# Stage two of a four-stage convolution and state-space kernel: chunks of 128 and 64 channels, norm factors through DRAM, B products on two engines

## The chip, the core and the metric

The kernel runs on one core of a Trainium2 chip. The metric is device time in microseconds; the time before is the median of three runs. A core has five engines with a queue of their own each: TensorE (PE, with its weight loads listed as PEld), VectorE (DVE), ScalarE (ACT), GpSimd (POOL) and SyncE (SP), which here issues the DMAs. A queue is worked off in order, so an instruction that waits holds up those behind it.

## The reference, cut to what matters

Four layers follow each other on an image batch of 4 x 192 x 64 x 64, all in f32. Layer 0 is a pair of Mambas, layer 1 (stage two of the kernel) is the one that the change touches, layers 2 and 3 are a dynamic depthwise convolution and a windowed mixing layer (stage three).

```python
def _mamba(xf, ...):                        # 384 inner channels, 16 states
    xm, z = split(xf @ in_proj_w.T)
    xm = silu(causal_depthwise_conv(xm, taps=3))
    dt, B, C = split(xm @ x_proj_w.T)       # 12, 16, 16
    delta = softplus(dt @ dt_proj_w.T + dt_proj_b)
    A = -exp(A_log)
    h = exp(delta * A) * h + (delta * xm) * B      # a scan over the 4096 positions
    y = (h * C).sum(states) + xm * Dskip
    return (y * silu(z)) @ out_proj_w.T

def _L1_conv_ref(x, ...):
    t = _ln(x, over the 192 channels)
    x1 = x + _mamba(t)
    dw = depthwise_conv_3x3(x1)
    x2 = x1 + gelu(batch_norm(dw))
    t = _ln(x2, over the 192 channels)
    h = gelu(t @ mlp_w1.T + mlp_b1)         # 768 hidden channels
    return x2 + h @ mlp_w2.T + mlp_b2
```

## The kernel before

The kernel has three stages. `two_mambas` is layer 0, `mamba_block` is layer 1, and `conv_and_windows` is layers 2 and 3; the end of stage two overlaps with the beginning of stage three. The first two stages are written on the same classes, `Mamba`, `Scans` and `Behind`.

**Units and tiles.** Stage two works in 32 units, 4 images of 8 tiles of T = 512 positions (8 rows of an image). The 192 channels lie as two chunks of CP = 96 on 96 partitions each: a tile of x is [96, 2, 512], and every product over channels is two products of 96 rows, added in PSUM, or gives two outputs of 96 rows.

**The scan.** A unit has 384 x 16 = 6144 state rows, that is 12 groups `k` of 4 tiles of 128. `Scans.step` issues one tile after the other, 48 in a unit, and between two tiles gives `Behind.tick` the turn. For a group: `load` fetches dtE and dtxE from DRAM in four broadcasts each (`load` is called 8 or 12 tiles ahead); `product` multiplies dtxE by B, one instruction of 128x2048, on DVE with B in PSUM (L561); `decay` makes dA = exp(A dt) on ACT in PSUM, two tiles ahead (L568); `step` is the scan on DVE (L574); `read` saves the state after the group's last tile (on POOL, L589) and multiplies h by C on POOL (L590); `sum` adds over the states on PE with outputs of 32 rows, four side by side (L599). There are three buffers of h, so DVE's product for a group waits until the sum of the third group before it is done. In stage one `shared = (3, 7, 11)` makes three of the twelve products on POOL instead, from a copy of B in SBUF (`Bs`), into buffers of their own (`h_apart`), copies the state on ACT, and lets the sums come two tiles later. In stage two `shared` is empty.

**The planner.** `Behind` places the rest of a unit's work between the scan tiles. It has four lanes of generators that yield a `Piece`: its estimated PE time, how many ticks to wait, what must be done before, whether it needs a PSUM bank (there are two, `BANKS`), whether it is a burst on ACT (allowed at the end of a group before a DVE product), and a lock shared by the two norms. Each tick may spend up to 2.1 us of PE work in stage two. What comes out of PSUM is issued one tick (ACT) or two ticks (DVE) after its product. So the program's order on every engine is fixed when the kernel is built.

**The work of a unit.** Lane 1 has `front` of the next unit (in_proj, L452; the convolution of 3 taps as products, L470; x_proj, L486; dt, L496, softplus, dt times xc on POOL, L506, and the stores to DRAM; z) and then `norm` of the one after. Lane 0 has `back`: out_proj (L1011), the addition of x on DVE (L1020) into a strip with a border, [96, 2, 10, 66]. Lane 2 has `tail`: the 3x3 convolution as nine products with diagonal weights per chunk (L1049), batch norm on the way out of PSUM (L1058), Gelu, the addition of x1 on POOL (L1072), and the second norm. Lane 3 has `end`: the MLP (L359, L364, L378) and the last addition (L1084) with its sums for stage three.

**The norm** (`NormT.run`): PE makes the mean on all partitions, DVE subtracts it (L292), ACT squares, PE makes the variance of 128 positions at a time as a column [128, 4] (L304), ACT and POOL raise it to the power -1/2 (L315, L316), PE spreads it over the partitions with the identity (`rb`, L322), DVE multiplies (L330), ACT applies gain and offset (L337).

Of the kernel before, what the change touches and what calls it, by code (L numbers as in the profile page):

```python
# [21 lines left out]
NB = 4  # L22
C = 192
# [70 lines left out]

def paired(a):

    return np.stack([a[:128], np.concatenate([a[128:], a[128:]]), a[:128]], axis=1)
# [67 lines left out]
class Piece:  # L165
# [4 lines left out]
    def __init__(self, pe=0.0, wait=0, after=(), burst=False, bank=False, lock=False):  # L170
        self.pe, self.wait, self.after, self.burst = pe, wait, after, burst
        self.bank, self.lock = bank, lock


class Behind:
# [39 lines left out]
    def try_lane(self, n, edge, force=False, idle=True):  # L215
# [7 lines left out]
        if not all(h[0] for h in p.after) or (p.bank and self.held >= self.BANKS):  # L223
            return None
# [44 lines left out]
class NormT:  # L269


    FIRST = dict(pe=1.7, bank=True)

    def __init__(self, nc, const, work, behind):
        self.nc, self.work, self.behind = nc, work, behind
        self.mean_w = const.tile([CP, CP], F32, name="mean_w")
# [8 lines left out]
    def run(self, x, g, b, d, which):  # L285
        nc, behind = self.nc, self.behind
        nq = T // 128
        mean = behind.bank([CP, T], "mean")
        for k in range(2):
            nc.tensor.matmul(mean, self.mean_w, x[:, k, :], start=(k == 0), stop=(k == 1))  # L290
        h = behind.later(
            lambda: nc.vector.tensor_tensor(  # L292
                d, x, mean.unsqueeze(1).broadcast_to([CP, 2, T]), ALU.subtract
# [4 lines left out]
        sq = self.work.tile([CP, 2, T], F32, name="ln_sq", bufs=1)  # L298
        nc.scalar.activation(sq, d, AF.Square)
        yield Piece(2.5, wait=2, bank=True)  # L300
        var = behind.bank([128, nq], "var")
        for q in range(nq):
            for k in range(2):
                nc.tensor.matmul(  # L304
                    var[:, q : q + 1],
                    sq[:, k, bass.ts(q, 128)],
                    self.mean_w[:, 0:1],
# [3 lines left out]
        behind.locked = False  # L311
# [7 lines left out]
        yield Piece(1.3, after=[h], wait=4, bank=True)  # L319
        rb = behind.bank([CP, T], "rb")  # L320
        for q in range(nq):
            nc.tensor.matmul(  # L322
                rb[:, bass.ts(q, 128)],
                rs[:, q : q + 1].to_broadcast([128, CP]),
                self.ident,
                start=True,
                stop=True,
            )
        h = behind.later(
            lambda: nc.vector.tensor_tensor(  # L330
                d, d, rb.unsqueeze(1).broadcast_to([CP, 2, T]), ALU.mult
            ),
            dve=True,
        )
        yield Piece(after=[h], wait=3)
        for k in range(2):
            nc.scalar.activation(  # L337
                d[:, k, :], d[:, k, :], AF.Identity, scale=g[:, k : k + 1], bias=b[:, k : k + 1]
            )


class MlpT:


# [4 lines left out]
    def run(self, x, taken, last):  # L349
        nc, behind = self.nc, self.behind  # L350
        made = []
        for m in range(NH):
# [1412 lines left out]
```

## Time and profile before

| | us |
|---|---|
| median of three runs (10863.65 to 10865.74) | 10863.88 |
| the profiled execution | 10868.44 |
| its span | 10866.7 |
| busy: PE | 9179.8 (84%) |
| busy: DVE | 9098.4 (84%) |
| busy: POOL | 7032.3 (65%) |
| busy: ACT | 6566.6 (60%) |

These are means over stages with different limits, so they are read by stage: stage one ends at about 5340 us, stage two's scans run from 5435 to 8957 us, and stage three goes on to the end. In a line of a group of instructions stand the line of the code, the engine, the operation, what is written and read, the count, then busy time and mean ns of one, then the engine's idle time just before them with what ended it. PEclk is the share of TensorE's full clock that was granted.

### The profile page before, as it was taken

The page shows a single profiled execution, that of the slowest core. Times are in us where ns is not written, and L with a number is a line of the kernel's source. Part 1 is how long each engine was busy: PE and PEld are TensorE (multiplying, and loading weights), DVE is VectorE, ACT ScalarE, POOL GpSimd, SP SyncE. Part 2 cuts the span into 40 slices and gives each one's busy share as a digit, 9 for nine tenths or more (in the row PEclk, how much of TensorE's full clock was granted, in tenths as well). Part 3 has the DMA queues.
Part 4 walks back from the last instruction along what each step waited for, and adds up shares of the span by engine and source line. Part 5 has one row for each costly group of instructions (what it writes and reads, how often), then busy time and mean ns, then how long its engine had stood idle before and what let it go on. Part 6 is the DMA issues. An engine that isn't in the chain of part 4 may idle for free. (4 is left out here: it accounts for less than half of the span.)

```text
span 10866.7 us, 97590 instructions
## 1 busy us (share of the span) xinstructions
PE 9179.8 (84%) x31352; PEld 3644.1 (34%) x31352; DVE 9098.4 (84%) x7962; ACT 6566.6 (60%) x9784; POOL 7032.3 (65%) x2688
## 2 busy tenths in 40 slices
PE   6888878888887887887679999999999987889898
PEld 2222222222322222222223333333333333455555
DVE  7999999999999999999698888888888885555552
ACT  5666666666666666666466666656666663444443
POOL 5888888888888888888666656656656661111100
PEclk7777777777777777777678889889889887999999
DMA  5666666666666666666454545445444443122110
GB/s 158 177 181 180 177 177 183 175 176 182 177 177 179 177 178 179 176 178 180 128 151 135 140 127 143 133 125 141 129 134 133 133 121 82 41 50 64 42 40 18
DMA packets 969560, 1515.13 MB, mean 139 GB/s; under 512 B 244346, under 2 KB 277150, under 8 KB 968534
## 3 DMA queue, kind: packets, MB, share of 16 engines
q1 hardware_dynamic: 968190, 1505.85, 51.4%
q8 instruction: 247, 4.05, 0.2%
q10 hardware_dynamic: 856, 3.05, 0.1%
q14 instruction: 267, 2.19, 0.1%
HBM read 1295.45 MB, written 213.12 MB: 139 GB/s over the span
## 5 line engine op out<-in xcount | busy, mean ns | idle before, releaser
L574 DVE TENSOR_TENSOR_SCAN h<-dA,m_state,h 128x512 f32<-128x512 f32 x3840 | 4668.9, 1266 | 487.4 <-ACT dA L568 422.7
L590 POOL TENSOR_TENSOR h<-h,C 128x2048 f32<-128x2048 f32 x960 | 4345.4, 4531 | 621.6 <-ACT m_state L587 480.7
L568 ACT ACTIVATE dA<-dtE,m_A 128x512 f32<-128x512 f32 x4608 | 3106.1, 687 | 1332.9 <-DVE h L574 1227.8
L561 DVE TENSOR_TENSOR h<-dtxE,B 128x2048 f32<-128x2048 f32 x960 | 2170.6, 2261 | 78.6 <-DMA dtxE<-r_dtx 65.9
L599 PE MATMUL y<-h,gather 128*32 128x512 f32 x7680 | 1281.3, 746 | 422.9 <-POOL h L590 345.2
L452 PE MATMUL ps_in<-xT,m_in_w 96*128 96x512 f32 x1536 | 939.5, 759 | 258.6 <-ACT raw L455 127.1
L1300 POOL TENSOR_TENSOR d<-d,rs 128x512 f32<-128x512 f32 x64 | 86.8, 1357 | 1589.7 <-DVE rs L1299 1569.1
L470 PE MATMUL ps_conv<-raw,m_conv 128*128 128x512 f32 x2112 | 989.3, 617 | 1.7 <-ACT xc L475 1.7
L574 DVE TENSOR_TENSOR_SCAN h_apart<-dA,m_state,h_apart 128x512 f32<-128x512 f32 x768 | 922.3, 1260 | 40.0 <-ACT dA L568 40.0
L590 POOL TENSOR_TENSOR h_apart<-h_apart,C 128x2048 f32<-128x2048 f32 x192 | 870.2, 4532 | 39.7 <-ACT m_state L587 38.0
L561 POOL TENSOR_TENSOR h_apart<-dtxE,Bs 128x2048 f32<-128x2048 f32 x192 | 889.6, 4633 | 6.0 <-ACT Bs L550 6.0
L452 PEld LDWEIGHTS ps_in<-xT,m_in_w 96*128 96x128 f32 x1536 | 351.3, 241 | 827.2 <-issue 420.5
L589 POOL COPY m_state<-h 128x4 f32<-128x4 f32 x384 | 72.3, 188 | 849.5 <-DVE h L574 813.5
L470 PEld LDWEIGHTS ps_conv<-raw,m_conv 128*128 128x128 f32 x2112 | 417.9, 202 | 599.0 <-issue 562.4
L1049 PE MATMUL ps_dw<-strip,dw 96*96 96x512 f32 x1152 | 578.7, 650 | 1.3 <-ACT x L1058 0.9
L599 PEld LDWEIGHTS y<-h,gather 128*32 128x32 f32 x7680 | 164.7, 117 | 1225.4 <-POOL h L590 552.0
L506 POOL TENSOR_TENSOR raw<-dt,xc 128x1536 f32<-128x1536 f32 x96 | 330.0, 3437 | 294.6 <-ACT dt L505 294.6
L486 PE MATMUL ps_x<-xc,m_pack 128*44 128x512 f32 x576 | 351.0, 758 | 199.5 <-ACT xc L482 194.6
L1465 PE MATMUL sed_ps<-xn,sed 64*128 64x256 f32 (+3 forms) x2944 | 485.9, 404 | 7.0 <-DVE y L1484 7.0
L568 ACT ACT_TABLE_LOAD x345 | 442.6, 1283 | 28.5 <-DMA dtE<-r_dt 22.3
L452 PE MATMUL ps_in<-xn,m_in_w 96*128 96x512 f32 x768 | 399.0, 666 | 47.4 <-ACT z L455 31.2
L378 PE MATMUL ps_o<-hid,t 128*96 128x512 f32 x768 | 390.4, 647 | 34.3 <-ACT hid L371 13.0
(193 smaller groups left out, 12217.1 us busy)
## 6 DMA issues: line engine op xcount, KB each, us to landing
dtE<-r_dt SPq DMA_DIRECT2D x2304, 256.0 KB, 5.0
dtxE<-r_dtx SPq DMA_DIRECT2D x2304, 256.0 KB, 4.1
r_dt<-dt SPq DMA_DIRECT2D x96, 768.0 KB, 4.0
r_dtx<-raw SPq DMA_DIRECT2D x96, 768.0 KB, 5.4
x<-x SPq DMA_DIRECT2D x64, 384.0 KB, 3.9
img<-x SPq DMA_DIRECT2D x28, 512.0 KB, 8.2
xt<-in_x SPq DMA_DIRECT2D x32, 384.0 KB, 5.8
x<-o SPq DMA_DIRECT2D x32, 384.0 KB, 5.0
```

Of the source, the lines that this page charges most:

```text
L378: nc.tensor.matmul(ps, self.w2[:, m, bass.ts(k, CP)], h[:, m, :], start=(m == 0), stop=(m == NH - 1),)
L452: nc.tensor.matmul(ps, self.in_w[:, k, bass.ts(e, 128)], xn[:, k, :], start=(k == 0), stop=(k == 1))
L470: nc.tensor.matmul(ps, self.conv[:, d, j, :], raw[:, d, j : j + T], start=(j == 0), stop=(j == K - 1))
L486: nc.tensor.matmul(ps, self.x_w[:, d, :], xc[:, d, :], start=(d == 0), stop=(d == ND - 1))
L506: nc.gpsimd.tensor_tensor(dtx, dt, xc, ALU.mult)
L561: engine.tensor_tensor(h, u["rows", k // 2, 1], u[B, k % 2].unsqueeze(1).broadcast_to([128, 4, T]), ALU.mult)
L568: self.nc.scalar.activation(dA, u["rows", k // 2, 0][:, j, :], AF.Exp, scale=self.A[:, k, j : j + 1])
L574: self.nc.vector.tensor_tensor_scan(h[:, j, :], u.pop(("dA", k, j)), h[:, j, :], self.state[:, k, j : j + 1], ALU.mult, ALU.add,)
L590: nc.gpsimd.tensor_tensor(h, h, u["C", k % 2].unsqueeze(1).broadcast_to([128, 4, T]), ALU.mult)
L599: self.nc.tensor.matmul(u["ys"][32 * j : 32 * j + 32, :], self.ex.gather[:, i // 2, :], h[:, j, :], start=(i == 0), stop=(i == 3 and not s ...
L1049: nc.tensor.matmul(ps, dw[:, k, j, :], s[:, k, dy : dy + rows, dx : dx + HW], start=(j == 0), stop=(j == 8),)
L1465: nc.tensor.matmul(out, sed[p, int(h is not None), i ^ position(k, s), cols], xn[b, g][p, c, :], start=group(t) not in begun, stop=left[gr ...
```

## The change

All of it is in stage two, but for the layout of three small inputs of stage three (the sums, `pooled` and `w1`, which follow the new chunks).

- The channels lie in chunks of 128 and 64. Inputs of a product hold the second chunk twice, on partitions 0 to 63 and on 64 to 127, so that two products over it can run on the two halves of the rows (`side_by_side`: in_proj, mlp1). Outputs and images hold it folded: the first 256 positions on partitions 0 to 63 and the others on 64 to 127 (`narrow`: out_proj, mlp2; the 3x3 convolution takes 256 columns for that chunk). A pair takes both PSUM banks at once, and `Piece.bank` becomes a number.
- The norm works in place. Its factors go from POOL to DRAM as a row of 512 and come back broadcast to 128 partitions; POOL multiplies by them instead of DVE, and the lock is held until then.
- `shared` is (3, 7, 11) with `folds=True`: POOL makes three of twelve B products, into one buffer of h_apart; the state is copied on ACT, and the sums come two tiles later. D, the gate and the skip stay as they were in stage two.
- x is loaded with its second chunk twice, into two buffers, after `front`; `back` loads x again, folded, into the strip and adds out_proj's result to it. Four small copies on ACT fill the border of the folded half. x2 goes to DRAM folded and comes back as xn with its second chunk twice.

```diff
 class NormT:
...
-        behind.locked = False
         rs = self.work.tile([128, nq], F32, name="ln_rs", tag=f"ln_rs{which}", bufs=1)
...
         h = behind.later(power)
-        yield Piece(1.3, after=[h], wait=4, bank=True)
-        rb = behind.bank([CP, T], "rb")
-        for q in range(nq):
-            nc.tensor.matmul(
-                rb[:, bass.ts(q, 128)],
-                rs[:, q : q + 1].to_broadcast([128, CP]),
-                self.ident,
...
+        yield Piece(after=[h], wait=4)
+        row = self.dram.tile([1, T], F32, name="r_rs", bufs=3)
+        nc.sync.dma_start(row.rearrange("o (q p) -> p (o q)", p=128), rs)
+        yield Piece(wait=2)
+        rb = self.work.tile([128, T], F32, name="rb", bufs=1)
+        nc.sync.dma_start(rb, row.broadcast_to([128, T]))
+        yield Piece(wait=2)
+        nc.gpsimd.tensor_tensor(x, x, rb.unsqueeze(1).broadcast_to([128, 2, T]), ALU.mult)
+        behind.locked = False
+        yield Piece(wait=3)
...
+def side_by_side(nc, outs, wts, x):
+    for o, wt in zip(outs, wts):
+        nc.tensor.matmul(o, wt[:, 0, :], x[:, 0, :], start=True, stop=False)
+    for i, (o, wt) in enumerate(zip(outs, wts)):
+        p = slice(64 * i, 64 * i + 64)
+        nc.tensor.matmul(o, wt[p, 1, :], x[p, 1, :], start=False, stop=True)
+
+def narrow(nc, ps, wt, x, k, start, stop):
+    if k == 0:
+        nc.tensor.matmul(ps, wt[:, :128], x, start=start, stop=stop)
+        return
+    for i in range(2):
+        nc.tensor.matmul(
+            ps[64 * i : 64 * i + 64, :], wt[:, 128:], x[:, bass.ts(i, T // 2)], start=start, stop=stop
+        )
...
     def product(self, u, k):
         apart = k in self.shared
         if apart:
-            h = self.work.tile([128, 4, T], F32, name="h_apart", bufs=2)
+            h = self.work.tile([128, 4, T], F32, name="h_apart", bufs=1 if self.folds else 2)
...
         mamba = Mamba(
-            nc, "m", 3, m_in, const, work, fixed, scan, psum_y, psum_a, dram, ln.ident, ex, behind
+            nc, "m", 3, m_in, const, work, fixed, scan, psum_y, psum_a, dram, ln.ident, ex, behind,
+            (3, 7, 11), True,
         )
...
+        STRIP = ((0, rows), (rows + 2, rows // 2))
+        PART = (slice(0, T), slice(T, T + T // 2))
+        def thrice(dma, a, k):
+            for p, ch, of in ((slice(0, 128), slice(0, 128), None), (half[0], slice(128, C), 0), (half[1], slice(128, C), 1)):
+                rows_of = a[ch, :] if k == 0 or of is None else a[ch, bass.ts(of, T // 2)]
+                dma(p, int(of is not None), rows_of)
...
         def front(u):
-            yield from mamba.front(u["xn"], u["t"] == 0, u["m"])
+            yield from mamba.front(u["x"], u["t"] == 0, u["m"])
+            if u["next"]:
+                load(u["next"])
...
         def back(u):
-            s = strips[b, t] = work.tile([CP, 2, rows + 2, HW + 2], F32, name="strip", bufs=3)
+            s = strips[b, t] = work.tile([128, 3 * rows // 2 + 4, HW + 2], F32, name="strip", bufs=3)
+            thrice(
+                lambda p, k, r: nc.sync.dma_start(
+                    inner(s, k)[p], r.rearrange("p (r c) -> p r c", c=HW)
+                ),
+                a,
+                1,
             )
...
                         lambda k=k, ps=ps: nc.vector.tensor_tensor(
-                            s[:, k, 1 : rows + 1, inside],
-                            ps.rearrange("p (r c) -> p r c", c=HW),
-                            u["x"][:, k, :].rearrange("p (r c) -> p r c", c=HW),
-                            ALU.add,
+                            inner(s, k), inner(s, k), ps.rearrange("p (r c) -> p r c", c=HW), ALU.add
                         ),
...
             yield Piece(after=made)
+            nc.scalar.copy(s[half[1], at, inside], s[half[0], at + n, inside])
+            nc.scalar.copy(s[half[0], at + n + 1, inside], s[half[1], at + 1, inside])
...
-            yield Piece(1.7, bank=True, wait=4, after=[taken[0]])
-            xn = work.tile([CP, 2, T], F32, name="xn2", tag="xn2", bufs=1)
-            yield from ln.run(x2, w["ln2_g"], w["ln2_b"], xn, 2)
+            yield Piece(wait=3)
+            r = dram.tile([C, T], F32, name="r_x2", bufs=2)
+            thrice(lambda p, k, a: nc.sync.dma_start(a, x2[p, PART[k]]), r, 1)
+            yield Piece(wait=2, after=[taken[0]])
+            xn = work.tile([128, 2, T], F32, name="xn2", bufs=1)
+            thrice(lambda p, k, a: nc.sync.dma_start(xn[p, k, :], a), r, 0)
+            yield Piece(1.7, bank=True, wait=2)
+            yield from ln.run(xn, w["ln2_g"], w["ln2_b"], 2)
...
-            u["next"] = units[n + 3] if n + 3 < len(units) else None
+            u["next"] = units[n + 2] if n + 2 < len(units) else None
```

## The prediction

> **What bounds the kernel now.** The chain of waits does not help: it ends in stage three and covers 5% of the span. I therefore read the engines' busy time stretch by stretch, found the stage the change touches, and then asked of that stage the groups of instructions, the waits and the order of time. Stage two starts with the first scan at 5435 us and its last scan ends at 8957 us; the second line below is stage two and the first a piece of stage one, which runs the same scans in another mixture.
>
> ```profile
> 2000.00:5000.00 3000.00, 2457.42 (x7600) 843.36 (x7600) 2919.41 (x2347) 2042.26 (x3295) 2650.95 (x737) 0.77 0.65 178
> ...
> 5435.00:8957.00 3522.00, 3195.92 (x9560) 1179.48 (x9560) 2978.04 (x2319) 2220.83 (x2944) 2179.55 (x1170) 0.88 0.49 134
> ```
>
> The columns are stretch, length, busy time (and instructions) of PE, PEld, DVE, ACT and POOL, granted clock, DMA share, GB/s. Stage two has 32 units (4 images of 8 tiles of 512 positions), so one unit lasts 3522/32 = 110.1 us and keeps PE busy for 99.9, DVE for 93.1, ACT for 69.4, POOL for 68.1 and the DMA engines for 0.49 x 110.1 = 54 us. Two engines are nearly full, PE the fuller. In stage one DVE is 97% busy beside a POOL at 88%: the scans can run that tight where PE has room.
>
> ```profile
> L574 DVE TENSOR_TENSOR_SCAN h<-dA,m_state,h 128x512 f32<-128x512 f32 x1525 | 1871.9, 1268 | 384.7 <-ACT dA L568 358.7 <-DVE h L561 0.5
> L590 POOL TENSOR_TENSOR h<-h,C 128x2048 f32<-128x2048 f32 x381 | 1726.3, 4531 | 30.8 <-POOL m_state L589 0.2
> L561 DVE TENSOR_TENSOR h<-dtxE,B 128x2048 f32<-128x2048 f32 x381 | 861.2, 2260 | 12.7 <-PE y L599 12.7
> L330 DVE TENSOR_TENSOR xn<-xn,rb 96x1024 f32<-96x1024 f32 x61 | 73.2, 1199 | 11.0 <-PE rb L322 11.0
> L364 ACT ACTIVATE hid<-ps_h,t 128x512 f32<-128x512 f32 x178 | 121.1, 684 | 145.3 <-PE ps_h L359 145.3
> L1058 ACT ACTIVATE x<-ps_dw,bn_t,bn_s 96x512 f32<-96x512 f32 x60 | 46.4, 773 | 155.6 <-PE ps_dw L1049 155.6
> ```
>
> These are groups of 5455 to 8955 us (31.8 units): busy, mean ns, idle before. DVE's idle time, 110.1 - 93.1 = 17.0 us a unit, is mostly 358.7/31.8 = 11.3 us before scans that wait for ACT's dA; and ACT is late because in its queue stand copies out of PSUM that wait for PE (145.3 and 155.6 in these two rows alone, 9.5 us a unit). So the end of a unit is set by PE and DVE together, with ACT between.
>
> ```profile
> 6513.60 5.45 PE L452 MATMUL ps_in<-xn,m_in_w 96*128 96x512 f32 x12
> ...
> 10206.08 1.66 PE L1275 MATMUL mean<-x,ones 128*128 128x256 f32 x8
> ...
> 10208.30 2.81 PE L1551 MATMUL ps_o<-hid,t_bw 128*64 128x256 f32 x24
> ```
>
> In the order of time, a product in f32 is two passes. Twelve passes of 512 columns take 5.45 us; the weight loads between them are 0.43 us apart, which is the pass at full clock. Stage three already packs as the change does: 24 passes of 128*64 with 256 columns take 2.81 us, 12 x 0.215 = 2.58 and 0.23 more, so two run at once. The mean has four passes of 128 rows and four of 64 rows: six turns of 0.215 make 1.29, and 0.37 is left for two changes of tile shape, 0.15 to 0.19 each.
>
> **What the Trainium skill says.** (1) TensorEngine Tiling (Array Packing), Key Properties: different tiles work in parallel, and changing the tiling mode drains the engine. The three lines above agree, at 0.15 to 0.19 us a change. (2) The same page, Gotcha 1: row tiles write to different PSUM banks; here a pair therefore takes both of the two banks. (3) SBUF — State Buffer, Who interferes with whom: a DVE instruction with two SBUF inputs contends with GpSimd's reads. Scans and B products read one operand from PSUM, and the scan takes 1260 to 1266 ns in stage one beside a full POOL against 1268 here, so a fuller POOL should not slow DVE. (4) DMA: Bandwidth & Descriptors, Rules for kernel authors: a DMA that reads what another wrote waits for that one's semaphore. So the factors' way through DRAM is two landings in series; the trace has no such pair of this size.
>
> **Part by part, a unit.** DVE loses 3 B products (3 x 2.26 = 6.8) and the two multiplications by rb (2 x 1.20 = 2.4). The last addition of back and of end has 256 columns instead of 512: half of 0.69 and of 0.73, 0.7 together. DVE: 93.1 - 9.9 = 83.2.
>
> POOL gains 3 B products at stage one's 4.635 (13.9), two multiplications of 128x1024, half of L590's 4.531 (4.5), and loses 12 copies of the state at 0.188 (2.3) and half of one L1072 of 1.18 (0.6). POOL: 68.1 + 15.5 = 83.6. That is now as much as DVE.
>
> ACT gains the 12 state copies at stage one's 0.196 (2.4), one copy of Bs (0.585) and four small strip copies (nearest row, POOL's at 0.29: 1.2); its eviction of dw and its Gelu shrink by 0.6. ACT: 69.4 + 3.6 = 73.0, hidden as work; a state copy waits for its scan, though, with copies and dA queued behind it, and POOL's read waits for the copy (in stage one 480.7 + 38.0 us over 64 units, 8.1 each).
>
> PE, in products of 512 columns (0.86 at full clock): in_proj 12 to 10, mlp1 12 to 9, mlp2 12 to 9, out 6 to 4.5, dw 18 to 13.5, rb 2 to 0, Bs 0 to 1: 15 fewer, 12.9 us. It gains changes of tile shape: about 24 in the packed groups and 14 in the two variances, whose products now alternate between 128 and 64 rows, at 0.15: 5.7. Net 7.2 at full clock, 8.2 at the stage's 0.88. PE: 99.9 - 8.2 = 91.7. Bounds: 12.9/0.88 = 14.7 if the changes cost nothing, 0 if they cost twice as much and half of the packing fails.
>
> The pairs (three in mlp1, two in in_proj) take both banks, so PE cannot fill one while ACT empties the other: up to one eviction and one dA, 0.68 + 0.68, five times, 6.8 us. Gathers stand in between, so I put 1.7 on the path; bounds 0 and 6.8.
>
> DMA gains 128 KB for x, 384 for the strip, 384 + 512 for x2's way out and in, 2 x 256 for rb: 1.9 MB at this stage's 54 us per 14.7 MB is 7.0, and some 2 more for the strip's rows of 256 B. 63 of 102 us is 62%, below stage one's 65%: hidden. SP issues 15 more transfers a unit (x 2, strip 3, x2 3, xn 3, out 2, row 2, rb 2). A load of dtE takes SP 0.6 us, so 9 us on top of some 31: hidden as work. But SP waits in order: the row's store waits for POOL's pow, rb waits for the row, x2's store for POOL's addition, with the next dtE and dtxE loads behind each. Those are issued 8 to 12 tiles ahead (over 16 us) and land in 4 to 5 us, so a wait of up to 10 is covered. Beyond that, ACT's dA is late and DVE stops.
>
> The row and rb have no row. Nearest landings: 2.6 and 3.3 (kept out and back) up to 5.4 and 5.0 (r_dtx, dtE), so 5.9 to 10.4 us from the pow to the multiplication. In POOL's queue, between the two, one read (4.5) stands for one norm and three large instructions (over 13 us) for the other. POOL waits 1.4 to 5.9 for the first, nothing for the second. I take 4: POOL 87.6, inside the unit.
>
> Sum: DVE 83.2, its waits of 17.0 as before (PE, which makes ACT late, falls by about as much as DVE, while POOL and the state copies give back what PE's extra room would bring), plus 1.7: 101.9, so 8.2 less, times 32 = 262. The ends grow: the first norm before the first scan has two more landings less the rb matmuls and DVE's multiplication, 8; the last tail some 7, partly beside stage three. Stages one and three are the same work. The profiled execution took 10868.4 us, 1.7 more than its span and 4.6 above the median of the runs, so that difference decides nothing: 10868.4 - 262 + 15 = 10621, rounded to 10625.
>
> **Rivals.** *DVE-bound.* As in stage one, waits nearly vanish; then POOL with 83.6 + 8.1 = 91.7 sets the unit: 18.4 x 32 = 589 less, plus 15: 10295. For it: PE's quiet stretches after in_proj's z. Against: PE's own 91.7 leaves nothing, and half clock returns whenever it pauses.
>
> *PE not relieved.* The drains and the bank pairs eat the packing (6.8 plus twice 5.7): PE stays near 100 and a unit near 107: 98 less, plus 15: 10785. For it: many short groups between gathers. Against: stage three's 2.81.
>
> *POOL becomes the bound: the slower side.* One mechanism: the multiplication by rb stands in POOL's in-order queue, and behind it stand the reads that the sums and the h buffers wait for. If POOL has no other work left when it gets there, both norms expose a whole trip: 83.6 + 8.1 + 2 x 8.5 + 4.4 (strip copies that wait for DVE, 138.3/31.8) = 113.1 a unit, 3.0 more: +97 + 15, 10980. It decides once POOL waits over 26.5 us a unit. For it: every filler of POOL's wait has the same queue, and SP's loads stand behind its late pow. Against: POOL now idles 42 us a unit, mostly for scans (787.8/31.8 = 24.8), and that idle time absorbs first.
>
> *No effect* would need the gains to be given back just so.
>
> **How the numbers follow.** Forecast 0.45 (units of 98.5 to 105: 10515 to 10725), PE not relieved 0.17, DVE-bound 0.08, POOL-bound 0.25, within 0.2% (22 us, about what a measurement of this kernel tells from no change) 0.05. Faster 0.70, same 0.05, slower 0.25. The range runs from 10400, leaving most of the DVE-bound case out, to 10980, the middle of the slower one.
>
> **What would show it.** DVE near 83 us busy a unit, POOL near 84, PE near 92; the packed lines at 128*64 with half their former time; POOL's idle time before the x<-x,rb row near 4 us a unit. I am wrong if that row or POOL's reads carry over 15 us of waiting a unit, if scans wait for dA over 17 us, if dA waits for DMA, or if the scan itself takes longer than 1.27 us.

## The result and the profile after

The kernel after takes 11152.3 us (11151.8 to 11154.1), 1.0265 times the kernel before, with an interval of 1.0247 to 1.0283: 287 us slower than the 10864.8 of the runs of before that were timed beside it, where 10625 was forecast. Stage two is where it went. Its scans run from 5442 to 9197 us, so the line by stretches that answers to those of before is this one of the kernel after:

```profile
5442.00:9197.00 3755.00, 3185.86 (x9652) 1163.54 (x9652) 2681.71 (x2160) 2275.31 (x3469) 2649.32 (x950) 0.80 0.60 142
```

A unit lasts 3755/32 = 117.3 us in place of 110.1; the stage takes 3755 - 3522 = 233 of the 287 us. The other 50 or so are at its ends: in the two profiled executions the first scan comes 7 us later, and from the last scan to the end of the kernel pass 1956 us in place of 1910. The work is what the prediction said: DVE is busy 83.8 us a unit (forecast 83.2), POOL 82.8 (83.6), ACT 71.1 (73.0), and PE has 99.6 us at a mean clock of 0.80. As an estimate, busy time times mean clock, that is 79.7 us at full clock against 87.9 before: 8.2 less (forecast 7.2). No engine is full. What grew is waiting: DVE idles 117.3 - 83.8 = 33.5 us a unit in place of 17.0. The groups of after, over 5462 to 9195 us (31.8 units), in the columns of those of before:

```profile
L594 DVE TENSOR_TENSOR_SCAN h<-dA,m_state,h 128x512 f32<-128x512 f32 x1143 | 1389.2, 1266 | 398.3 <-ACT dA L588 385.2 <-DVE h L581 0.5
L610 POOL TENSOR_TENSOR h<-h,C 128x2048 f32<-128x2048 f32 x287 | 1296.6, 4518 | 383.7 <-ACT m_state L607 370.3 <-DMA dtxE<-r_dtx 13.2
...
L581 DVE TENSOR_TENSOR h<-dtxE,B 128x2048 f32<-128x2048 f32 x285 | 644.2, 2260 | 0.0
L594 DVE TENSOR_TENSOR_SCAN h_apart<-dA,m_state,h_apart 128x512 f32<-128x512 f32 x383 | 474.5, 1268 | 247.6 <-ACT dA L588 196.9 <-POOL h_apart L581 50.7
...
L610 POOL TENSOR_TENSOR h_apart<-h_apart,C 128x2048 f32<-128x2048 f32 x95 | 429.9, 4526 | 91.3 <-ACT m_state L607 91.3
...
L330 POOL TENSOR_TENSOR x<-x,rb 128x1024 f32<-128x1024 f32 x31 | 73.2, 2361 | 337.3 <-DMA rb<-r_rs 302.1 <-PE var L309 22.4 <-PE y L619 12.8
...
L330 POOL TENSOR_TENSOR xn<-xn,rb 128x1024 f32<-128x1024 f32 x29 | 68.7, 2368 | 26.1 <-DMA rb<-r_rs 25.9 <-issue 0.2
```

The scan and the B product cost the same as before, each. The idle time before the two rows of scans is (398.3 + 247.6)/31.8 = 20.3 us a unit, where it was 12.1. POOL waits (337.3 + 26.1)/31.8 = 11.4 us for the factors, and (383.7 + 91.3)/31.8 = 14.9 us before its reads, put down to the state's copy on ACT (before, it waited longer, but for the scans themselves). Most of the rest of DVE's idle time is in the view of waits of the same stretch (engine, line, what it waited for: us in total, times, longest):

```profile
DVE strip L1065 <- PE ps_out L395: 180.5, 31, 6.5
...
DVE xn L297 <- PE mean L295: 165.5, 30, 8.4
```

The addition into the strip and the second norm's subtraction hold DVE's queue for 5.7 and 5.2 us a unit, with scans behind them. Before, the same addition and both norms' subtractions waited for 2.2 and 0.4 (groups of 5455 to 8955 us):

```profile
L292 DVE TENSOR_TENSOR xn<-x,mean 96x1024 f32<-96x1024 f32 x60 | 72.3, 1204 | 12.3 <-PE mean L290 12.3
...
L1020 DVE TENSOR_TENSOR strip<-ps_out,x 96x512 f32<-96x512 f32 x62 | 42.4, 685 | 69.0 <-PE ps_out L1011 69.0
```

What makes them late is seen in the order of time, here one unit of after (start us, length; in brackets the idle time before):

```profile
7050.17 1.03 POOL L320 TENSOR_TENSOR ln_rs<-ln_rs,minus_half 128x4 f32<-128x4 f32 x1
...
7051.23 0.38 SPq L325 DMA_DIRECT2D r_rs<-ln_rs  x1
...
7061.09 0.33 SPq L328 DMA_DIRECT2D rb<-r_rs  x1
...
7069.31 2.37 POOL L330 TENSOR_TENSOR x<-x,rb 128x1024 f32<-128x1024 f32 x1 [11.69 <-DMA rb<-r_rs]
...
7077.22 4.54 POOL L581 TENSOR_TENSOR h_apart<-dtxE,Bs 128x2048 f32<-128x2048 f32 x1
...
7081.79 1.28 DVE L594 TENSOR_TENSOR_SCAN h_apart<-dA,m_state,h_apart 128x512 f32<-128x512 f32 x1 [3.14 <-POOL h_apart L581]
...
7086.16 1.27 POOL L652 TENSOR_TENSOR m_y<-m_y,z 128x512 f32<-128x512 f32 x1
...
7087.48 2.07 PE L395 MATMUL ps_out<-m_y,m_pack 128*128 128x512 f32 x2 [4.39 <-POOL m_y L652]
...
7089.60 0.69 DVE L1065 TENSOR_TENSOR strip<-strip,ps_out 128x512 f32<-128x512 f32 x1 [6.52 <-PE ps_out L395]
...
7091.30 0.69 ACT L499 ACTIVATE xc<-ps_conv,m_pack 128x512 f32<-128x512 f32 x1 [10.30 <-PE ps_conv L494]
```

From the pow to the multiplication pass 19 us, 11.7 of them with POOL idle. Behind it in POOL's queue stand the B product, for which a scan then waits, and the gate; for the gate waits the projection out, for that DVE's addition, and ACT waits for a convolution that stands behind the projection in PE's queue. In this unit one late multiplication stops four engines. The landings say why the trip is long (KB each, median us from issue to landing):

```profile
rb<-r_rs SPq DMA_DIRECT2D x61, 256.0 KB, 6.3
...
r_rs<-ln_rs SPq DMA_DIRECT2D x61, 2.0 KB, 9.4
```

The smallest transfer of the stage, 2 KB, takes the longest of all to land: 9.4 us. DMA: Bandwidth & Descriptors, Rules for kernel authors, in the Trainium skill says that a strided last dimension becomes one descriptor for each element; the row's store, with neighbours in a partition 128 positions apart in DRAM, is of that kind: 512 pieces of 4 bytes. The packets agree: from 6000 to 8000 us the core moves 61586 packets under 512 bytes, and 49410 in a kernel below whose rows go out in 128 pieces each (e7). (34 rows with 384 pieces less each make 13056.)

### The profile page after: what moved, and what is told of

Its sections match the earlier page's. It is cut to its first block, busy times and chain, and to the rows that moved or that the text cites. A ratio compares the mean times of both kernels' runs of the same rounds, so it can differ in the third digit from the quotient of the medians.

```text
span 11152.3 us, 98827 instructions
## 1 busy us (share of the span) xinstructions
PE 9157.2 (82%) x31480; PEld 3630.1 (33%) x31480; DVE 8799.5 (79%) x7802; ACT 6627.2 (59%) x10322; POOL 7501.6 (67%) x2472
## 5 line engine op out<-in xcount | busy, mean ns | idle before, releaser
L594 DVE TENSOR_TENSOR_SCAN h<-dA,m_state,h 128x512 f32<-128x512 f32 x3456 | 4183.9, 1265 | 499.0 <-ACT dA L588 447.1
L610 POOL TENSOR_TENSOR h<-h,C 128x2048 f32<-128x2048 f32 x864 | 3907.2, 4527 | 995.2 <-ACT m_state L607 910.7
L581 DVE TENSOR_TENSOR h<-dtxE,B 128x2048 f32<-128x2048 f32 x864 | 1952.6, 2260 | 86.3 <-DMA dtxE<-r_dtx 86.3
L594 DVE TENSOR_TENSOR_SCAN h_apart<-dA,m_state,h_apart 128x512 f32<-128x512 f32 x1152 | 1397.7, 1262 | 286.1 <-ACT dA L588 235.2
L610 POOL TENSOR_TENSOR h_apart<-h_apart,C 128x2048 f32<-128x2048 f32 x288 | 1304.5, 4529 | 141.1 <-ACT m_state L607 139.4
L581 POOL TENSOR_TENSOR h_apart<-dtxE,Bs 128x2048 f32<-128x2048 f32 x288 | 1316.2, 4570 | 7.6 <-issue 5.6
L558 PE MATMUL B<-dbl,spread 44*128 44x512 f32 x384 | 319.1, 926 | 182.9 <-DVE h L581 182.9
L619 PE MATMUL y<-h_apart,gather 128*32 128x512 f32 x2304 | 383.0, 743 | 84.0 <-POOL h_apart L610 84.0
L1093 PE MATMUL ps_dw<-strip,dw 128*128 128x256 f32 (+1 forms) x1152 | 443.1, 535 | 0.0
L385 PE MATMUL ps_in<-x,m_in_w 128*128 128x512 f32 x384 | 261.3, 800 | 187.9 <-ACT hid L362 97.8
```

What stands on the lines that cost most here:

```text
L558: self.nc.tensor.matmul(B, self.ex.spread[:, o, :], u["dbl"], start=True, stop=True)
L581: engine.tensor_tensor(h, u["rows", k // 2, 1], u[B, k % 2].unsqueeze(1).broadcast_to([128, 4, T]), ALU.mult)
L594: self.nc.vector.tensor_tensor_scan(h[:, j, :], u.pop(("dA", k, j)), h[:, j, :], self.state[:, k, j : j + 1], ALU.mult, ALU.add,)
L610: nc.gpsimd.tensor_tensor(h, h, u["C", k % 2].unsqueeze(1).broadcast_to([128, 4, T]), ALU.mult)
L619: self.nc.tensor.matmul(u["ys"][32 * j : 32 * j + 32, :], self.ex.gather[:, i // 2, :], h[:, j, :], start=(i == 0), stop=(i == 3 and self. ...
L1093: nc.tensor.matmul(ps, dw[:, k, j, :], s[:, at + dy : at + dy + n, dx : dx + HW], start=(j == 0), stop=(j == 8),)
```

## The experiments

Three theories at first: (1) the factors' trip through DRAM; (2) what comes with POOL's B products (state's copy on ACT, later sums, fewer edges for bursts); (3) the pairs that take both PSUM banks. Each run was timed beside runs of the kernel before on the same chip; the ratio is to those. In the texts on record "after" is the changed kernel.

| kernel | us | ratio to before, interval |
|---|---|---|
| after | 11152 | 1.0265 (1.0247 to 1.0283) |
| e1: factors through TensorE | 10842 | 0.9977 (0.9968 to 0.9986) |
| e2: no B products on POOL | 10968 | 1.0090 (1.0075 to 1.0105) |
| e3: e1 and e2 together | 10775 | 0.9912 (0.9897 to 0.9927) |
| e4: no pairs | 11233 | 1.0335 (1.0320 to 1.0350) |
| e5: after, state's copy on POOL | 11061 | 1.0176 (1.0161 to 1.0192) |
| e6: e1, state's copy on POOL | 10718 | 0.9861 (0.9846 to 0.9875) |
| e7: after, row in pieces of 16 bytes | 11033 | 1.0150 (1.0135 to 1.0166) |
| e12: e7, state's copy on POOL | 11009 | 1.0127 (1.0110 to 1.0144) |
| e18: e12, chain two ticks shorter | 10916 | 1.0049 (1.0033 to 1.0065) |
| e11: e1, chain four ticks longer | 11023 | 1.0120 (1.0082 to 1.0158) |
| e15: e11 and dense products | 10906 | 1.0034 (1.0022 to 1.0047) |
| e8: after, both multiplications four ticks later | 11364 | 1.0453 (1.0436 to 1.0471) |
| e9: after, first multiplication two ticks later | 11063 | 1.0175 (1.0160 to 1.0191) |
| e10: e7, multiplication on DVE | 11134 | 1.0244 (1.0229 to 1.0259) |
| e13, e14: after and dense products | 11132, 11118 | 1.0243 (1.0228 to 1.0259), 1.0230 (1.0215 to 1.0245) |
| e16: e12 and dense products | 11024 | 1.0143 (1.0126 to 1.0160) |
| e17: e6 and dense products | 10726 | 0.9865 (0.9851 to 0.9880) |

### Which part: e1 to e4

e1 puts the factors back on the way they had before; the lock is released after the variance again.

```diff
-        row = self.dram.tile([1, T], F32, name="r_rs", bufs=3)
-        nc.sync.dma_start(row.rearrange("o (q p) -> p (o q)", p=128), rs)
...
-        nc.gpsimd.tensor_tensor(x, x, rb.unsqueeze(1).broadcast_to([128, 2, T]), ALU.mult)
+        yield Piece(1.3, after=[h], wait=4, bank=True)
+        rb = behind.bank([128, T], "rb")
+        for q in range(nq):
+            nc.tensor.matmul(rb[:, bass.ts(q, 128)], rs[:, q : q + 1].to_broadcast([128, 128]), self.ident, start=True, stop=True)
+        h = behind.later(
+            lambda: nc.vector.tensor_tensor(x, x, rb.unsqueeze(1).broadcast_to([128, 2, T]), ALU.mult), dve=True
+        )
```

> After, with only the norms' factors taken back through TensorE and VectorE (small products into a PSUM bank, the multiplication by VectorE, the lock released after the variance). Theory 1 (the factors' trip through DRAM, about 15 to 18 us from the pow to GpSimd's multiplication, holds GpSimd's queue, so the gate, the projection out and the scans behind the strip's addition come late): 10,750 to 10,950 us, although VectorE gets two multiplications a unit more. Theory 2 (GpSimd's B products, state copies on ScalarE, sums two ticks later) and theory 3 (pairs that take both PSUM banks at once): 11,100 to 11,300 us, since neither is touched and VectorE has more to do.

10842 us: 310 less than after, in theory 1's range, though DVE is busy 86.3 us a unit in place of 83.8.

e2 makes all B products on DVE.

```diff
-            (3, 7, 11), True,
+            (), True,
```

> After, with all 12 B products of stage two on VectorE again, the state copy on GpSimd, the sums at the old tick and an edge for every group; chunks, pairs and the norm through DRAM stay. Theory 2 (the shared products make GpSimd and ScalarE late): 10,800 to 11,000 us. Theory 1 or 3: 11,050 to 11,300 us; under theory 1 a little below after is possible, since GpSimd has 3 products less behind the held multiplication, with VectorE about 7 us a unit more.

10968 us: 184 less, in theory 2's range. Both are at work. e3 makes both edits:

> Both undone together: chunks of 128 and 64 channels with pairs and the folded image alone are left of the change. Theory 1 and 2 together explain all: 10,700 to 10,870 us, no slower than before, since TensorE has about 7 us a unit less at full clock. Theory 3 (pairs and the folded image cost the time): 11,000 to 11,250 us.

10775 us, faster than before by 0.9%. Its stage two by stretches:

```profile
5432.00:8851.00 3419.00, 2973.11 (x10092) 1172.05 (x10092) 2957.11 (x2319) 2226.81 (x3058) 2163.56 (x1179) 0.86 0.58 151
```

A unit of 106.8 us with PE busy for 92.9. So the chunks, pairs and folded image are worth 95 us; on top of them the DRAM trip alone costs 193 (e2 less e3), POOL's products as made here 67 (e1 less e3), and both together 377: 117 more than the two sums. One thing in the traces comes only with both. The store of dt for the next unit is issued after 24 of a unit's 48 scans in e1 and e2, and nearly always in e3, but after 32 in after. In e2, with the whole DRAM trip, it stands here, 54 us after its unit's first scan at 6998.1:

```profile
7052.39 0.38 SPq L535 DMA_DIRECT2D r_dt<-dt  x1
```

What that place is worth comes further down; what each part does on POOL comes first.

e4 takes each output of a pair for itself.

```diff
-            groups = [[0, 1], [2]] if self.folds else [[d] for d in range(ND)]
+            groups = [[d] for d in range(ND)]
...
-    FIRST = dict(pe=2.9, bank=2)
+    FIRST = dict(pe=1.7, bank=1)
-        for m in range(0, NH, 2):
+        for m in range(NH):
```

> After, with each output of the projection in and of the MLP's first layer in its own piece and one bank (no two outputs side by side; both chunks' products one after the other); chunks, norm through DRAM and shared products stay. TensorE gets 5 products of 512 columns a unit more. Theory 3 (both banks taken at once stall TensorE and ScalarE): 10,850 to 11,050 us in spite of that. Theory 1 or 2: 11,150 to 11,350 us.

11233 us, 81 slower than after, with five products more a unit: theory 3 falls. Here the pairs pay for their banks.

### What in POOL's products: e5 and e6

```diff
-        if self.shared:
+        if self.shared and not self.folds:
             nc.scalar.copy(self.state[:, k, :], h[:, :, T - 1])
```

> After, with the state's copy (12 a unit, 0.19 us each) back on GpSimd and nothing else changed. Theory 2a (the copy in ScalarE's queue, behind whatever stands there, is what makes GpSimd's reads late: 11 us of GpSimd's idle a unit is put down to it in after): 10,950 to 11,080 us. Theory 2b (the read waits for the scan anyway, and the wait only changes its name; the costs of the shared products are their 4.5 us on GpSimd, the sums and the edges): 11,110 to 11,200 us.

> The kernel with the factors through TensorE again (10,842 us), with the state's copy on GpSimd as well. Theory 2a: 10,690 to 10,790 us, below chunks alone (10,775). Theory 2b: 10,810 to 10,900 us.

11061 and 10718 us: 91 and 124 less than after and e1. 2b's guess that the wait would only change its name fails. In e1 the waits between 6000 and 8000 us (18.1 units) are led by POOL's reads:

```profile
POOL h_apart L618 <- ACT m_state L615: 268.4, 54, 6.7
...
POOL h L618 <- ACT m_state L615: 204.7, 36, 9.1
```

In e6, in the same stretch (18.8 units), the place that took over is the copy on POOL itself:

```profile
POOL m_state L617 <- DVE h L602: 203.1, 74, 6.4
```

and 74.3 us before the copies of h_apart: 277 in place of 473 us. POOL's B product, which did not wait in e1, now waits 74.0 us, so 122 us are saved in sum. The place of the copy is a cause. How it costs is read from the queues and not tested apart: in ACT's queue it stands behind evictions that wait for PE, and makes POOL's reads late, and they the sums and the buffers. e6 is the fastest kernel of the study: with the copy on POOL, the B products there save 57 us (e3 less e6) where they had cost 67.

### What in the trip: e7, e8, e9, e10, e12

e7 lets a partition hold four neighbours, so that the row goes out in 128 pieces of 16 bytes.

```diff
-                    sq[p, k, bass.ts(q, 128)],
+                    sq[p, k, q:T:nq],
...
-        nc.sync.dma_start(row.rearrange("o (q p) -> p (o q)", p=128), rs)
+        nc.sync.dma_start(row.rearrange("o (p q) -> p (o q)", q=nq), rs)
```

> After, with the variance's columns taken from every fourth position, so that a partition holds four neighbours and the row goes out in 128 pieces of 16 bytes in place of 512 of 4 bytes. Its store landed after a median of 8.2 to 9.4 us in after; all else of the trip stays. Theory 1a (the length of the trip, and in it the row of single elements, costs the time): store at 4 to 6 us, GpSimd's wait for the factors down from 9.5 us a unit to 4 to 6, time 10,950 to 11,080 us. Theory 1b (what costs is the multiplication on GpSimd, 2.4 us in place of 1.2 us on VectorE, or the lock; the trip's length does not matter): 11,110 to 11,170 us. A store no faster than before would leave both open.

11033 us, 119 less. In e7 the landings and POOL's wait for the first norm's factors are, from 6000 to 8000 us (17.2 units):

```profile
r_rs<-ln_rs SPq DMA_DIRECT2D x34, 2.0 KB, 3.8
```

```profile
L330 POOL TENSOR_TENSOR x<-x,rb 128x1024 f32<-128x1024 f32 x17 | 40.3, 2370 | 39.1 <-DMA rb<-r_rs 34.6 <-PE ps_Bs L569 4.5
```

The store takes 3.8 us in place of 9.4, and POOL waits 2.3 us a unit before the first multiplication in place of 10.6. The length of the trip counts (1a). The edit also has a price: it reads the variance's weights with a stride of 16 bytes, and their loads take longer in the same stretch, first in after and then in e7 (mean clocks of the two runs 0.80 and 0.81). So the shorter store alone may be worth more than the 119 us.

```profile
L309 PEld LDWEIGHTS var<-mean_w,ln_sq 128*128 128x128 f32 x266 | 53.4, 251 | 35.9 <-ACT dA L588 28.3 <-issue 6.2
```

```profile
L309 PEld LDWEIGHTS var<-mean_w,ln_sq 128*128 128x128 f32 x272 | 73.7, 319 | 36.3 <-ACT dA L588 28.3 <-issue 6.5
```

e8 leaves the transfers and puts the multiplication four ticks later.

```diff
-        yield Piece(wait=2)
+        yield Piece(wait=6)
         nc.gpsimd.tensor_tensor(x, x, rb.unsqueeze(1).broadcast_to([128, 2, T]), ALU.mult)
```

> After, with GpSimd's multiplication by the factors put into its queue six ticks after the factors' load in place of two (some 10 us later); the transfers are issued as before. Theory 1c (GpSimd's queue is held by the waiting multiplication, and the gate and the next B product stand behind it): GpSimd's wait for the factors falls under 2 us a unit and the time to 10,880 to 11,050 us. Theory 1d (the chain from the variance to the normed image is too long for the next unit's front, held or not): 11,150 to 11,350 us.

11364 us, although the first multiplication never waits: 1c fails here, but not cleanly. In the order that the planner writes, a unit's rows (the stores of dt and dtx, from which the next unit's scans live) stand after step 32 of 48 (a step is one scan tile) in after; the first load of them is due at step 36. e8 overran that in 31 units, and the planner then issues everything at once; in e8's trace the store of dt comes after 38 scans. So e9 moves the first norm's multiplication alone, by two ticks, which keeps the rows at step 32 (`wait=4 if which == 1 else 2`).

> After, with the first norm's multiplication alone put into GpSimd's queue two ticks later (four after the factors' load in place of two; some 5 us). In the order that the planner writes, the next unit's rows stay at step 32 of 48, as in after, with step 36 as the deadline; e8 had overrun it in 31 of 32 units, so that it was no clean test of the held queue. Theory 1c (what costs is GpSimd's queue held by the waiting multiplication): GpSimd's wait for the first norm's factors falls from 9.5 to about 5 us a unit and the time to 11,000 to 11,100 us. Theory 1d (length of the chain): 11,130 to 11,260 us.

11063 us, 90 less, in 1c's range; but the groups of e9 between 6000 and 8000 us (17.3 units) say that its reading was too simple:

```profile
L330 POOL TENSOR_TENSOR x<-x,rb 128x1024 f32<-128x1024 f32 x18 | 42.6, 2369 | 15.6 <-DMA rb<-r_rs 12.6 <-DMA dtxE<-r_dtx 3.0
L330 POOL TENSOR_TENSOR xn<-xn,rb 128x1024 f32<-128x1024 f32 x18 | 42.5, 2359 | 208.8 <-DMA rb<-r_rs 150.7 <-DMA dtE<-r_dt 58.2
```

The wait moved to the second norm; the sum, 224/17.3 = 13.0 us a unit, did not fall. What is gone is the first norm's wait, ahead of the B product and the gate. So the sum of POOL's waits does not set the price; as far as this one run shows, their place in the queue does.

e10 is e7 with the multiplication on DVE and three ticks in place of two (`nc.vector` for `nc.gpsimd`, `wait=3`).

> The kernel with the row in pieces of 16 bytes (11,033 us), its multiplication by the factors from SBUF on VectorE in place of GpSimd, three ticks after the factors' load in place of two. The trip through DRAM is the same. Theory 1b (the multiplication's place: 4.7 us a unit in GpSimd's full queue): 10,850 to 10,960 us. If the trip's remaining length is what costs: 11,000 to 11,150 us, VectorE now being the one that is held.

11134 us, 101 more than e7: to take the multiplication off POOL does not help here, and 1b's range is missed. 1b also named the lock, which is still held until the multiplication; no run tests it alone. e12 adds e5's edit to e7's.

> After with two repairs at once that gave 119 and 91 us alone: the row in pieces of 16 bytes and the state's copy on GpSimd; the factors still go through DRAM. If the two are separate losses: 10,930 to 10,960 us, and the trip's remainder is worth some 220 us beside the kernel with the factors through TensorE and the same copy (10,718 us). If they are the same loss seen twice: 11,010 to 11,050 us.

11009 us: 143 less than after, where 119 and 91 stood apart. Mostly the same loss seen twice. POOL hardly waits for the factors any more, nothing for the first norm's and this for the second's, from 6000 to 8000 us (17.3 units):

```profile
L330 POOL TENSOR_TENSOR xn<-xn,rb 128x1024 f32<-128x1024 f32 x17 | 40.2, 2367 | 4.5 <-DMA rb<-r_rs 4.5
```

Yet e12 is 291 us above e6, which differs only in the factors' way, with its ticks, lock, engine and the strided weights. So the held queue is not the main part of what the trip costs.

### The chain's place in the unit: e11 and e18

e11 is e1, without DRAM or POOL, with the chain as long as in after.

```diff
-        yield Piece(1.3, after=[h], wait=4, bank=True)
+        yield Piece(1.3, after=[h], wait=8, bank=True)
```

> The kernel with the factors through TensorE (10,842 us), with four ticks more between the pow and the products that spread it: the chain has the length in ticks that it has in after, and the next unit's rows come at step 32 as there, not at 24, but no transfer and nothing of GpSimd is in it. Theory 1d (the chain's length in the planner's order costs the time): 10,930 to 11,050 us. Theory 1c or 1b (GpSimd's held queue or its longer work): 10,830 to 10,890 us.

11023 us in the middle, 180 more than e1. Three of the four runs took 11023 to 11025 us and one 10934, 92 above e1; why the same kernel has both is open. So four ticks of waiting in the plan, with nothing of the DRAM trip in them, make more than half of the 310 us in three runs and a third in one. The plan's step is seen in the trace, at the store of dt in the order of time. In after it is

```profile
7134.32 0.38 SPq L535 DMA_DIRECT2D r_dt<-dt  x1
```

79 us after that unit's first scan at 7054.9, of 119.6 us; in e1 it is

```profile
6995.37 0.38 SPq L543 DMA_DIRECT2D r_dt<-dt  x1
```

53 us after its unit's first scan at 6942.0, of 112.5. In the planner's order that is step 32 against step 24, and the scans in the traces agree; before it was 24 to 28. Lane 1 holds front and norm one after the other, so a longer norm puts the next front later, and softplus, as a burst, then waits for the next edge, the end of a group before a product on DVE. With products 3, 7 and 11 on POOL step 28 is no such edge. That fits e2, where the chain is as long, all products are on DVE and the store stays at 24; the edges were not tested alone.

e18 asks the same with the DRAM trip left in: e12 with 2 + 1 + 3 ticks in place of 4 + 2 + 2, which puts the rows at step 24.

> The kernel with the row of 16 bytes and the state's copy on GpSimd (11,009 us, factors through DRAM, multiplication on GpSimd), with the planner's waits from the pow to the multiplication cut from 4 + 2 + 2 to 2 + 1 + 3 ticks. In the order that the planner writes, the next unit's rows then come at step 24 of 48 as in the kernels with the factors through TensorE, not at 32. Theory 1d (the place of the next unit's front in the unit is what the long chain costs): 10,800 to 10,900 us. Theory 1c (the trip and the held queue, not the place): GpSimd is held some 5 us more a norm, 11,000 to 11,150 us.

10916 us, 93 less than e12, some 16 above the upper end of 1d's range and far below 1c's. The stage by stretches, first e12 and then e18:

```profile
5436.00:9054.00 3618.00, 3200.61 (x9652) 1214.96 (x9652) 2677.89 (x2162) 2225.05 (x3086) 2720.19 (x1333) 0.82 0.57 148
```

```profile
5439.00:8962.00 3523.00, 3030.66 (x9656) 1177.83 (x9656) 2695.11 (x2162) 2235.55 (x3088) 2725.72 (x1334) 0.86 0.58 152
```

The same instructions; PE is busy 5.3 us a unit less, about what a clock of 0.86 in place of 0.82 makes, and a unit is 110.1 us in place of 113.1. From e18 to e6, whose rows also stand at step 24, 198 us are left. POOL waits 0.9 us a unit for the factors there (16.6 us in the 17.9 units from 6000 to 8000 us). What the 198 us consist of, the lock, the multiplication on POOL, two more ticks or the strided weights, no run takes apart.

### By what the place costs: e13 to e17

The stretches of one unit's last two groups of scans show TensorE full at half its clock in after, and not in e1. First after, then e1:

```profile
7156.20:7161.00 4.80, 4.80 (x19) 2.69 (x18) 4.80 (x6) 3.13 (x4) 4.80 (x2) 0.50 0.80 214
7161.00:7174.50 13.50, 13.50 (x26) 4.74 (x27) 8.20 (x8) 9.91 (x13) 11.60 (x5) 0.50 0.69 153
```

```profile
7035.40:7044.00 8.60, 8.60 (x23) 3.10 (x22) 6.58 (x7) 4.72 (x8) 8.60 (x2) 0.84 0.87 235
7044.00:7054.50 10.50, 10.02 (x53) 4.33 (x49) 8.76 (x10) 5.59 (x10) 7.89 (x4) 1.00 0.61 157
```

Theory 4: TensorE idles ahead (6.1 us before the B product at 7154.58), falls to half clock, and that makes the end of the unit long. The test puts products of 128 x 128 x 512 there that nothing reads.

```diff
+            ps = self.behind.psum.tile([128, T], F32, name="warm", tag="mm")
+            for d in range(n):
+                self.nc.tensor.matmul(ps, m.out_w[:, d % ND, :128], u["xc"][:, d % ND, :], start=True, stop=True)
```

> After, with five extra products of 128 x 128 x 512 a unit on TensorE ahead of the B product of step 41, where it idles 6 us; nothing reads their result. Theory 4a (the idle of TensorE brings the half clock for the last quarter of the unit, and that makes it long): clock in the last two of twelve groups 0.8 to 1.0 in place of 0.50, time 10,950 to 11,080 us although TensorE has 5 products more. Theory 4b (the clock is not the cause, or the sparse products behind bring it down again at once): 11,150 to 11,260 us.

> After, with three such products ahead of the B product and three more, one at a time, among the products behind it that use little of the array (sums into 32 columns, spreads of 44 rows, variances of one column), up to the unit's end. Theory 4c (TensorE's half clock stays because the products there are sparse, busy or not; dense ones among them bring the full clock back): clock in the last two groups over 0.8, time 10,930 to 11,060 us. Theory 4b: 11,150 to 11,280 us.

> The kernel with the factors through TensorE and four ticks more in the chain (11,023 us), with five such dense products a unit, two ahead of the B product of step 41 and three among those behind it. Theory 4 (what the long chain costs is the half clock at the unit's end): last two groups at 0.8 to 1.0 and 10,870 to 10,960 us. If the clock is a mere companion: 11,020 to 11,130 us.

11132, 11118 and 10906 us. Mean length in us and granted clock, over 26 units (the 5th to the 30th), of the last three groups of scans of a unit and the first two of the next, worked out from the scans' starts and the clock records:

```
        group 10    group 11    group 12    group 1     group 2
after   8.7 0.72    4.7 0.50    13.7 0.50   7.1 0.68    11.4 0.87
e13     8.7 0.99    4.7 0.65    13.5 0.50   7.1 0.61    11.6 0.90
e14     8.7 0.93    4.7 0.51    14.7 0.54   7.1 1.00    10.0 0.97
e11    12.4 0.67    4.7 0.50    13.2 0.50   7.1 0.50    12.4 0.82
e15    11.1 0.91    4.7 1.00    10.9 0.57   7.1 0.97    10.5 0.86
e16     8.7 0.96    4.7 0.58    14.6 0.53   7.2 0.95    12.9 0.81
e12     8.7 0.79    4.7 0.50    13.8 0.50   7.1 0.53    14.4 0.84
e18     8.1 0.50    7.4 0.85    12.4 0.91   8.0 0.63    12.6 0.95
```

In e11 five products more, whose result nothing reads, give back 116 of the 180 us: all six runs of e15 took 10899 to 10918 us. That speaks for the clock as a cause, since they do nothing else that could help; but group 12 became shorter by more than its clock rose (0.50 to 0.57), and one of e11's runs was only 28 us above e15 without them. In after they lifted the clock only around group 12, where TensorE is full at 0.50, not in it, and gave 20 and 35 us; for the 20 (e13) the intervals of the ratios overlap.

> The kernel with the row of 16 bytes and the state's copy on GpSimd (11,009 us), with six dense products a unit on TensorE around step 41, as in e14; nothing reads their result. Theory 4 (with GpSimd's waits gone the half clock at the unit's end is what is left of the long chain): 10,880 to 10,950 us. If the clock costs no more than it did in after itself (35 us): 10,960 to 11,000 us; if it is a companion: 11,010 to 11,080 us.

> The fastest kernel so far (factors through TensorE, state's copy on GpSimd: 10,718 us), with three dense products a unit in the stretch where TensorE has the half clock there (the tenth of twelve groups, clock 0.50). Theory 4: 10,640 to 10,700 us. If TensorE has enough room there at the half clock: 10,715 to 10,780 us.

e16 took 11024 us, 15 more than e12, with group 12 still at 0.53; e17 10726, no gain over e6. So for the kernels with the DRAM trip it stays open how much of the place's cost is the clock: dense products did not get it up in their group 12. In e18 it is up there, 0.91, and the group takes 12.4 us in place of e12's 13.8, but in e18 the place moved as well.

## Why the prediction was wrong

- **The work: right.** The sums of busy time of DVE, POOL and ACT came within 2 us of the forecast, and PE's work within 1 us at full clock. The tile shapes, half-length packed products, POOL's product (4.53 us, forecast 4.64) and the hidden DMA (0.60, forecast 62%) held; the scan stayed at 1.27 us, and dA hardly ever waited for a transfer.
- **"DVE 83.2, its waits of 17.0 as before": the step that failed.** They are 33.5. The sentence in brackets beside it, that PE's room and POOL's load cancel, was never derived. In e3, where the norms and POOL are left as they were, DVE idles 106.8 - 2957.11/32 = 14.4 us, and the step holds; POOL's products and the trip broke it. The prediction had named a sign for this, scans that wait for dA over 17 us a unit, and it came true: (385.2 + 196.9)/31.8 = 18.3.
- **The trip, 5.9 to 10.4 us.** It took 9.4 + 6.3 = 15.7 in landings alone. The term was sized by the landings of large transfers. POOL's wait was set at 4 us and measured 11.4; e7 shows that 119 us of the time are in the row's 4-byte pieces.
- **What stood behind the wait.** I counted POOL's wait as POOL's time, "inside the unit". In the unit shown the gate and the B product stand behind it, and PE, DVE and ACT wait for them in turn; with that one wait moved, 90 us come back (e9). It is not the main part: with hardly any wait left, e12 is still 291 us above e6.
- **A term that was missing.** The sum has no line for the planner's ticks: the norm's chain became four ticks longer and, beside POOL's products, moved the next unit's front from steps 24 to 28 to step 32. Without the trip that is worth 180 us in e11 (92 in one of its four runs), and 93 come back in e18.
- **The state's copy on ACT, "hidden as work".** The prediction saw that POOL's read waits for it and charged 8.1 us to a rival only. 91 us in after (e5), 124 in e1 (e6).
- **PE, "8.2 at the stage's 0.88".** By the estimate above the work fell by 8.2 us at full clock, but the clock fell to 0.80 with it, so PE's busy time stayed at 99.6.
- **The bank pairs, 1.7 of at most 6.8.** Not contradicted: without them the kernel is slower (e4).
- **The ends, +15.** It is some 50. Of the 46 us behind the last scan 35 are gone in e1, with the factors through TensorE.
- **The slower rival, 10980, decided by POOL waiting over 26.5 us a unit.** The right sign, and in part the right place, the multiplication in POOL's queue; but POOL is busy 82.8 of 117.3 us and idle 34.5. That is over 26.5, but says only that the unit grew, since busy and idle time always add up to it. POOL is not the bound, and the norms do not both expose a trip (10.6 and 0.8 us). POOL is late, not full, and that is dearer.

## What to carry to other kernels

Sums of busy time are the easy half of a forecast; before waits are set "as before", follow for each chain that grows what stands behind its waiting instruction in that queue, and on whom those wait in turn. Where the order is planned ahead, a longer chain can also move everything that follows it in its lane, deadline met or not: look at where the next unit's first stores land. And give each part of a change its own run: here the chunks won 95 us and POOL's products 57 more, and the detour of the norms' factors took 343 from them (e5 less e6).

## What the hardware showed

The row of 2 KB landed after 9.4 us in 512 pieces of 4 bytes and 3.8 in 128 of 16. TensorE stayed at half clock while the trace has it busy without a gap, 4.80 + 13.50 = 18.3 us in the two lines of after above. TensorE: Matmul & The Clock Gate, What's actually happening, in the Trainium skill has the full clock come back after about 3.4 us of sustained work; here it did not, and the products there are, beside a mean, mostly sums into 32 columns, spreads of 44 rows and variances of one column. That their sparseness is the reason was not shown: dense ones among them (e14) did not bring the clock back in that group, though they did in the next (1.00 in place of 0.68). And DVE's multiplication by factors from SBUF took 1.62 us for the first norm in e10 and 1.21 for the second, with the factors in PSUM 1.20 and 1.22 in e1; why the first is longer in e10 is open. A load of 128 x 128 weights from every fourth f32 took 0.32 us in e7, from neighbours 0.25 in after.
